# Window attention scores as 64x64 matmuls on quarters of the TensorE array: two heads per matmul in place of four

## The chip, the cores and the metric

The kernel runs on one core of one Trainium2 chip. The metric is device time in microseconds (us) of one execution; lower is better. Each kernel was run on the same chip, in the same rounds, as the kernel before. Engines are written as in the profile: PE is TensorE, PEld its weight loads, DVE VectorE, ACT ScalarE, POOL GpSimd. "Cold" means that the clock record of the trace shows a granted TensorE clock of 0.50, "warm" that it shows 1.00; the 264 records of the trace before have no other value. The 263 changes of the clock inside the span stand within 3 ns of a grid of 3413.33 ns; a step of that grid is called a clock window here, or a window.

## The reference

There are 32 images of 56x56 positions and 128 channels, all fp32. Two layers follow each other, each with a group norm in front and a residual around it.

```python
# layer 0: shifted-window attention, 64 windows of 7x7 = 49 tokens, 4 heads of 32
qkv  = (win @ w_qkv.T).reshape(-1, 49, 3, 4, 32)
attn = einsum('bhid,bhjd->bhij', q * 32**-0.5, k) + bias + shift_mask
out  = einsum('bhij,bhjd->bihd', softmax(attn), v) @ w_proj.T + b_proj
...
# layer 1: cosine transform along rows and along columns, 32 modes each with its own
# 128x128 matrix, transform back, sum; then a feed-forward 128 -> 512 -> 128
out_y = einsum('bixy,ioy->boxy', dct(x)[..., :32], w0)
...
h = relu(h @ W1 + b1) @ W2 + b2
```

## The kernel before

An image's attention goes by eight rows of eight windows. From the second image on it runs beside layer 1 of the image before; a scheduler decides the order of instructions on each engine. The scores use keys laid out block-diagonally: head h's keys stand in channels 32h to 32h+31 and in columns of their own, with zeros elsewhere, so one matmul on all 128 channels gives all four heads of a window.

```python
k_bd = big.tile([P, NWR, NH, WT], F32, ...)          # 128 x 8 x 4 x 49, zeros written once
...
for h in range(NH):                                  # 4 copies a row, two engines in turn
    hs = slice(h * HD, (h + 1) * HD)
    if h % 2: nc.vector.tensor_copy(k_bd[hs, :, h], pk3[hs])     # L244
    else:     nc.scalar.copy(k_bd[hs, :, h], pk3[hs])            # L246
...
for hf in range(2):
    ps = attn_bank()
    for w4 in range(4):
        w = 4 * hf + w4
        half = w % 2
        nc.tensor.matmul(                            # L270: scores
            ps[half * JP : (half + 1) * JP, ...],    # JP = 64: two windows, one per column half
            lhsT=q[:, w * WT : w * WT + JP],         # 128 x 64
            rhs=k_bd[:, w].rearrange("c h j -> c (h j)"),   # 128 x 196
            start=True, stop=True)
```

In layer 1 the part that matters is the mode matrices (L405), in a first group of 32 matmuls (with `w1sb`) and, later in the image, a second group (with `w0sb`). In front of each the group norm's shift is added to the constant mode, and in front of the second GpSimd adds a bias to a large tile:

```python
nc.vector.tensor_scalar(y[:, 0], y[:, 0], shift, None, ALU.add)             # L394
if width:                                                                    # second group only
    nc.gpsimd.tensor_tensor(xtok, xtok, b2sb..., ALU.add)                    # L396
for g in range(NM // 8):
    pz = conv_bank()
    for c in range(8):
        nc.tensor.matmul(pz[:, c * S : (c + 1) * S], lhsT=wmix[:, k], rhs=y[:, k], ...)   # L405
```

## Time and profile before

| kernel before | value | from |
|---|---|---|
| time | 6739.01 us, median of 3 (6730.82 to 6739.05) | first runs |
| profiled span, mean granted clock | 6717.8 us, 0.882 | profile |
| time with the clock at 0.50 | 1591 us | clock record |
| scores: 2048 matmuls, 4096 passes | 506.8 us busy, 272.2 us idle in front | groups |
| second mode groups that stay cold | 9 of 31 | timeline of TensorE |

The prediction shows the page's lines and the timeline. An fp32 matmul is recorded as two passes, so a count of x16 in a timeline is eight matmuls. The stall in front of the second mode group is in the timeline of all engines (start, us, engine, line, operation, tiles and shapes, count, and in brackets the idle time before with what ended it):

```profile
2716.82 7.73 POOL L396 TENSOR_TENSOR xtok<-xtok,b2sb 112x3584 f32<-112x3584 f32 x1 [6.26 <-PE pc L379]
2717.23 7.37 DVE L394 TENSOR_SCALAR y<-y,shift 128x56 f32<-128x56 f32 x1 [0.59 <-ACT y L388]
```

A VectorE addition on 56 elements a partition takes 7.37 us. The same instruction takes 250 ns at its fastest, ahead of the first mode group, where GpSimd does not run its large addition; here it lasts until that addition ends (2724.60 and 2724.55 us). TensorE waits for it, and the clock record falls to 0.50 at 2720.20 us.

### The profile page before, as it was taken

How to read it: one execution, taken by the hardware profiler on the slowest of the kernel's cores; microseconds unless marked ns; L12 is line 12 of the kernel's file. 1: busy time of each engine (PE TensorE's matmuls, PEld its weight loads, DVE VectorE, ACT ScalarE, POOL GpSimd, SP SyncE). 2: the span in 40 equal slices, each digit the busy share in tenths (PEclk: the TensorE clock that was granted, in tenths of full speed). 3: DMA queues.
4: the chain of work that ended last, by engine and by line, in shares of the span. 5: the costliest groups of instructions: out<-in, count | busy, mean ns of one | idle time of the engine just before them, and what ended most of it. 6: DMA issues, size and time to landing. Idle time of an engine off the chain costs nothing.

```text
span 6717.8 us, 106748 instructions
## 1 busy us (share of the span) xinstructions
PE 5716.7 (85%) x46336; PEld 4468.3 (67%) x46336; DVE 2547.3 (38%) x4263; ACT 2529.2 (38%) x4737; POOL 1637.8 (24%) x1614
## 2 busy tenths in 40 slices
PE   5888889888888888898888888888888888888888
PEld 3766667666667666676666766666766667666666
DVE  4343333333343433333333334334343333333331
ACT  2433334334334343343333343433433334334332
POOL 2222221222212222212222122222122221222210
PEclk8988889889898898898898998988988989889886
DMA  1000000000000000000000000000000000000000
GB/s 57 13 15 19 20 20 11 15 16 20 20 17 12 13 20 20 20 11 13 17 20 20 11 16 15 20 20 20 9 13 19 20 20 11 15 16 20 11 11 10
DMA packets 210798, 115.20 MB, mean 17 GB/s; under 512 B 7927, under 2 KB 209944, under 8 KB 210072
## 3 DMA queue, kind: packets, MB, share of 16 engines
q1 hardware_dynamic: 206136, 102.84, 5.9%
q8 instruction: 364, 5.96, 0.4%
q10 hardware_dynamic: 4192, 5.54, 0.2%
q14 instruction: 106, 0.87, 0.0%
HBM read 56.93 MB, written 51.38 MB: 16 GB/s over the span
## 4 chain that ended last, share of the span: by engine, by line
PE 68%; DVE 12%; POOL 9%; ACT 8%; issue 2%; DMA 0%; SPq 0%; ACTq 0%; POOLq 0%; DVEq 0%
PE pc L464 11%; PE pc L405 9%; PE pc L450 9%; PE pa L270 7%; PE pc L379 7%; PE pc L433 6%; POOL xw L218 6%; DVE y L394 4%; PE pa L329 3%; PE pa L316 3%; PE pa L306 3%; PE pa L239 2%; PE pa L236 2%; POOL t L288 2%; PE pa L251 2%
## 5 line engine op out<-in xcount | busy, mean ns | idle before, releaser
L288 POOL TENSOR_TENSOR t<-t,mx 128x784 f32<-128x784 f32 x256 | 384.2, 1501 | 3506.8 <-DVE mx L287 3506.8
L464 PEld LDWEIGHTS pc<-wff,hid 128*112 128x112 f32 x7168 | 844.2, 177 | 142.3 <-issue 69.3
L464 PE MATMUL pc<-wff,hid 128*112 128x128 f32 x7168 | 897.3, 275 | 1.8
L458 ACT ACTIVATE hid<-pc,b1sb 128x448 f32<-128x448 f32 x896 | 549.5, 632 | 686.7 <-PE pc L450 650.7
L270 PE MATMUL pa<-k_bd,q 128*64 128x196 f32 x4096 | 506.8, 380 | 272.2 <-DVE k_bd L244 272.2
L450 PE MATMUL pc<-xf,wff 128*128 128x448 f32 x1792 | 728.6, 541 | 0.0
L244 DVE COPY k_bd<-pa 32x392 f32<-32x392 f32 x512 | 289.5, 566 | 910.6 <-ACT k_bd L246 908.6
L296 POOL TENSOR_TENSOR a<-a,rs 128x784 f32<-128x784 f32 x256 | 388.6, 1518 | 826.9 <-DVE rs L295 561.0
L270 PEld LDWEIGHTS pa<-k_bd,q 128*64 128x64 f32 x4096 | 337.8, 157 | 359.1 <-DVE k_bd L244 267.1
L405 PE MATMUL pc<-y,w0sb 128*128 128x56 f32 x2048 | 380.1, 371 | 230.1 <-DVE y L394 230.1
L405 PEld LDWEIGHTS pc<-y,w0sb 128*128 128x128 f32 x2048 | 370.1, 284 | 253.3 <-DVE y L394 241.3
L312 DVE COPY aT<-pa 128x512 f32<-128x512 f32 x512 | 352.8, 689 | 471.2 <-PE pa L306 469.9
L277 DVE TENSOR_TENSOR t<-pa,bm 128x392 f32<-128x392 f32 x512 | 289.9, 567 | 630.0 <-PE pa L270 622.7
L316 PE MATMUL pa<-aT,v 128*64 128x49 f32 x8192 | 385.2, 239 | 120.1 <-DVE aT L312 120.1
L316 PEld LDWEIGHTS pa<-aT,v 128*64 128x64 f32 x8192 | 315.4, 149 | 250.1 <-DVE aT L312 134.0
L450 PEld LDWEIGHTS pc<-xf,wff 128*128 128x128 f32 x1792 | 318.6, 191 | 213.9 <-issue 208.1
L388 ACT ACTIVATE y<-pc,rstd 128x256 f32<-128x256 f32 x448 | 211.5, 472 | 613.0 <-PE pc L379 459.3
L472 DVE TENSOR_TENSOR xtok<-pc,xtok 112x512 f32<-112x512 f32 x224 | 154.4, 689 | 746.2 <-PE pc L464 746.2
L412 ACT COPY z<-pc 128x448 f32<-128x448 f32 x256 | 136.2, 532 | 779.0 <-PE pc L405 779.0
L306 PE MATMUL pa<-ident,a 128*128 128x128 f32 x2048 | 369.5, 306 | 48.0 <-POOL a L296 48.0
L334 DVE SCALAR_TENSOR_TENSOR xT<-pa,bproj,xT 128x371 f32<-128x371 f32 (+2 forms) x576 | 200.2, 394 | 492.5 <-PE pa L329 492.5
L218 POOL TENSOR_SCALAR xw<-xT,rstd,nb 128x343 f32<-128x343 f32 (+7 forms) x864 | 370.9, 450 | 11.9 <-DVE ve L174 11.5
(78 smaller groups left out, 8916.5 us busy)
## 6 DMA issues: line engine op xcount, KB each, us to landing
xload<-in_x_dram SPq DMA_DIRECT2D x64, 784.0 KB
out_dram<-xtok SPq DMA_DIRECT2D x224, 224.0 KB
w0sb<-in_w_dram ACTq DMA_DIRECT2D x1, 2048.0 KB
w1sb<-in_w_dram ACTq DMA_DIRECT2D x1, 2048.0 KB
wff<-in_W_dram ACTq DMA_DIRECT2D x2, 256.0 KB
rpb<-in_rpb_rev_dram ACTq DMA_DIRECT2D x25, 0.8 KB
rpb<-in_rpb_rev_dram SPq DMA_DIRECT2D x24, 0.8 KB
wqkv<-in_w_qkv_t_dram ACTq DMA_DIRECT2D x1, 192.0 KB
```

The source lines that it names most:

```text
L218: nc.gpsimd.tensor_scalar(xw[:, i, j0:j1, r0:r1, s0:s1], xT[:, y0 : y0 + r1 - r0, x0 : x0 + cols].rearrange("p r (j s) -> p j r s", s=s1 - ...
L270: nc.tensor.matmul(ps[half * JP : (half + 1) * JP, (w4 // 2) * NH * WT : (w4 // 2 + 1) * NH * WT], lhsT=q[:, w * WT : w * WT + JP], rhs=k_ ...
L288: nc.gpsimd.tensor_tensor(t3, t3, mx.unsqueeze(2).to_broadcast([P, NR, WT]), ALU.subtract)
L296: nc.gpsimd.tensor_tensor(a3, a3, rs.unsqueeze(2).to_broadcast([P, NR, WT]), ALU.mult)
L306: nc.tensor.transpose(pt[:, m * P : (m + 1) * P], a[:, pr, 2 * hp : 2 * hp + 2].rearrange("p h j -> p (h j)"), ident,)
L316: nc.tensor.matmul(po[hp * JP : (hp + 1) * JP, w * WT : (w + 1) * WT], lhsT=v[:, w, hp].rearrange("j h d -> j (h d)"), rhs=aT[:, 2 * (w4 / ...
L379: nc.tensor.matmul(py[:, c * 2 * NM : (c + 1) * 2 * NM], lhsT=tok[:, c], rhs=dct_sb, start=True, stop=True,)
L405: nc.tensor.matmul(pz[:, c * S : (c + 1) * S], lhsT=wmix[:, k], rhs=y[:, k], start=True, stop=True,)
L433: nc.tensor.matmul(px[:, c * NL : (c + 1) * NL], lhsT=zT[:, c], rhs=idct, start=True, stop=True)
L450: nc.tensor.matmul(ph[:, :GT], lhsT=wff1[:, f * P : (f + 1) * P], rhs=xf[:, 8 * g : 8 * g + 8].rearrange("p r w -> p (r w)"), start=True, ...
L458: nc.scalar.activation(hf, ph[:, :GT], AF.Relu, bias=b1sb[:, f : f + 1])
L464: nc.tensor.matmul(pf[:TC, c * C : (c + 1) * C], lhsT=hid[f][:, c * TC : (c + 1) * TC], rhs=wff2[:, f], start=(f == 0), stop=(f == NF - 1),)
```

## The change

The intent is to halve the array work of the scores. Heads 0 and 1 lie in channels 0 to 63, heads 2 and 3 in 64 to 127. A matmul on one half of the channels needs only two heads' columns: 64 rows, 64 columns of the array, 98 streamed columns. Two halves of the channels and two windows make four quarters of the array; that they work at the same time was not shown before the change, and is measured below (24 ns a pass on four quarters in turn, 43 on two). The keys shrink to 128 x 8 x 2 x 49, the scores of a head pair go to a PSUM bank of their own, and the bias tile, `t` and `a` are regrouped to fit. The numbers of copies, additions and softmax steps stay.

```diff
-    k_bd = big.tile([P, NWR, NH, WT], F32, tag="k_bd", name="k_bd")
+    k_bd = big.tile([P, NWR, 2, WT], F32, tag="k_bd", name="k_bd")
...
-        for hf in range(2):
-            ps = attn_bank()
-            for w4 in range(4):
-                w = 4 * hf + w4
-                half = w % 2
+        ps = [attn_bank(), attn_bank()]
+        for w in range(NWR):
+            for hp in range(2):
+                cs = slice(hp * JP, (hp + 1) * JP)
+                qs = slice((w % 2) * JP, (w % 2 + 1) * JP)
                 nc.tensor.matmul(
-                    ps[half * JP : (half + 1) * JP, (w4 // 2) * NH * WT : (w4 // 2 + 1) * NH * WT],
-                    lhsT=q[:, w * WT : w * WT + JP],
-                    rhs=k_bd[:, w].rearrange("c h j -> c (h j)"),
+                    ps[hp][qs, (w // 2) * 2 * WT : (w // 2 + 1) * 2 * WT],
+                    lhsT=q[cs, w * WT : w * WT + JP],
+                    rhs=k_bd[cs, w].rearrange("c h j -> c (h j)"),
                     start=True,
                     stop=True,
                 )
...
```

Cut: the layouts of the bias tile, `t`, `a` and the transposes of `a`, which follow from this, and comments. Line numbers move: scores L270 are L276 after, key copies L244/L246 are L248/L250, mode matrices L405 are L412, the shift's addition L394 is L401, attention times values L316 is L323.

More of the change, by code (lines that the diff above doesn't have):

```diff
@@ L121, in swin_fourier_kernel @@
     mask_sb = const_load([P, 2, 3, WT], shift_mask.rearrange("r s p j -> p r s j"), "mask")
-    bm = const.tile([P, 2, 3, NH, WT], F32, tag="bm", name="bm")
-    rpb_f = rpb.rearrange("p h y x -> p h (y x)")
+    bm = const.tile([P, 2, 2, NWR // 2, 2, WT], F32, tag="bm", name="bm")
+    rpb_f = rpb.rearrange("p (t h) y x -> p t h (y x)", t=2)
     for r in range(2):
-        for s in range(3):
-            nc.vector.tensor_tensor(
-                bm[:, r, s],
-                rpb_f,
-                mask_sb[:, r, s].unsqueeze(1).to_broadcast([P, NH, WT]),
-                ALU.add,
-            )
+        for pr in range(NWR // 2):
+            for t in range(2):
+                nc.vector.tensor_tensor(
+                    bm[:, r, t, pr],
+                    rpb_f[:, t],
+                    mask_sb[:, r, 0 if pr < NWR // 2 - 1 else 2]
+                    .unsqueeze(1)
+                    .to_broadcast([P, 2, WT]),
+                    ALU.add,
+                )
     dct_sb = const_load([TC, 2 * NM], dct, "dct")
@@ L151, in swin_fourier_kernel @@
         v_bd.append(big.tile([P, NWR, 2, 2, HD], F32, tag=f"v{i}", name=f"v{i}"))
-        a_sb.append(big.tile([P, NWR // 2, NH, JP], F32, tag=f"a{i}", name=f"a{i}"))
+        a_sb.append(big.tile([P, 2, NWR // 2, 2, JP], F32, tag=f"a{i}", name=f"a{i}"))
         nc.gpsimd.memset(q_sb[i], 0.0)
@@ L243, in attn_scores @@
             if h % 2:
-                nc.vector.tensor_copy(k_bd[hs, :, h], pk3[hs])
+                nc.vector.tensor_copy(k_bd[hs, :, h % 2], pk3[hs])
             else:
-                nc.scalar.copy(k_bd[hs, :, h], pk3[hs])
+                nc.scalar.copy(k_bd[hs, :, h % 2], pk3[hs])
         pv = attn_bank()
@@ L263, in attn_scores @@
             )
-        t = work.tile([P, 2, 2, NH * WT], F32, tag="t", name="t")
-        for hf in range(2):
-            ps = attn_bank()
-            for w4 in range(4):
-                w = 4 * hf + w4
-                half = w % 2
+        t = work.tile([P, 2, RT], F32, tag="t", name="t")
+        ps = [attn_bank(), attn_bank()]
[3 more added lines that the diff above has]
+                qs = slice((w % 2) * JP, (w % 2 + 1) * JP)
                 nc.tensor.matmul(
-                    ps[half * JP : (half + 1) * JP, (w4 // 2) * NH * WT : (w4 // 2 + 1) * NH * WT],
-                    lhsT=q[:, w * WT : w * WT + JP],
-                    rhs=k_bd[:, w].rearrange("c h j -> c (h j)"),
+                    ps[hp][qs, (w // 2) * 2 * WT : (w // 2 + 1) * 2 * WT],
+                    lhsT=q[cs, w * WT : w * WT + JP],
+                    rhs=k_bd[cs, w].rearrange("c h j -> c (h j)"),
                     start=True,
@@ L276, in attn_scores @@
                 )
+        for hp in range(2):
             nc.vector.tensor_tensor(
-                t[:, hf],
-                ps[:, : 2 * NH * WT].rearrange("p (a m) -> p a m", a=2),
-                bm[:, i // (NWR - 1), hf : hf + 2].rearrange("p a h j -> p a (h j)"),
+                t[:, hp],
+                ps[hp][:, :RT],
+                bm[:, i // (NWR - 1), hp].rearrange("p a h j -> p (a h j)"),
                 ALU.add,
@@ L283, in attn_scores @@
         NR = NWR // 2 * NH
-        t3 = t.rearrange("p f a (h j) -> p (f a h) j", h=NH)
-        a3 = a.rearrange("p a h j -> p (a h) j")[:, :, 0:WT]
+        t3 = t.rearrange("p t (m j) -> p (t m) j", j=WT)
+        a3 = a.rearrange("p t a h j -> p (t a h) j")[:, :, 0:WT]
         mx = small.tile([P, NR], F32, tag="mx", name="mx")
@@ L307, in attn_out @@
                     pt[:, m * P : (m + 1) * P],
-                    a[:, pr, 2 * hp : 2 * hp + 2].rearrange("p h j -> p (h j)"),
+                    a[:, hp, pr].rearrange("p h j -> p (h j)"),
                     ident,
```

## The prediction

> **What bounds the kernel now.** I read the page first (engines, granted clock, chain that ended last), then the groups by shape, then TensorE's instructions in order of time over several images. The kernel handles 32 images; from the second on, an image's attention runs beside the previous image's Fourier layer and feed-forward.
>
> ```profile
> PE   5888889888888888898888888888888888888888
> PEclk8988889889898898898898998988988989889886
> PE 68%; DVE 12%; POOL 9%; ACT 8%; issue 2%; DMA 0%; SPq 0%; ACTq 0%; POOLq 0%; DVEq 0%
> L270 PE MATMUL pa<-k_bd,q 128*64 128x196 f32 x4096 | 506.8, 380 | 272.2 <-DVE k_bd L244 272.2
> L251 PE MATMUL pa<-wqkv,xw 128*49 128x64 f32 x8192 | 322.4, 229 | 0.0
> L316 PE MATMUL pa<-aT,v 128*64 128x49 f32 x8192 | 385.2, 239 | 120.1 <-DVE aT L312 120.1
> ```
>
> TensorE is the bound: 68% of the chain, busy nearly everywhere. The scores (L270) hold 7% of the chain, some 470 us; that is the ceiling of what the change can touch. The second row matters as much: the mean granted clock is 0.882. Read microsecond by microsecond it is only ever 0.50 or 1.00, and 1591 us of the span (about 49 us an image) are at 0.50. The page's last column of L270 says TensorE also stood idle 272 us in front of it, waiting for the key copies.
>
> The timeline of TensorE shows where the clock comes back:
>
> ```profile
> 2724.66 7.07 PE L405 MATMUL pc<-y,w0sb 128*128 128x56 f32 x32 [7.17 <-DVE y L394]
> 2731.66 2.60 PE L270 MATMUL pa<-k_bd,q 128*64 128x196 f32 x14
> 2734.19 3.78 PE L405 MATMUL pc<-y,w0sb 128*128 128x56 f32 x32
> ...
> 3752.36 7.07 PE L405 MATMUL pc<-y,w0sb 128*128 128x56 f32 x32 [7.17 <-DVE y L394]
> 3759.37 2.88 PE L270 MATMUL pa<-k_bd,q 128*64 128x196 f32 x14
> 3762.17 7.08 PE L405 MATMUL pc<-y,w0sb 128*128 128x56 f32 x32
> ...
> 6631.52 13.90 PE L405 MATMUL pc<-y,w0sb 128*128 128x56 f32 x64 [7.96 <-DVE y L394]
> ```
>
> (Start, us, instructions; an fp32 matmul is recorded as two passes.) Each image TensorE idles 7.2 us for the shift (DVE, L394) and the clock falls to half. Sixty-four passes of the mode matrices follow; 14 score passes stand in their middle. In 22 of the 31 images with attention the second 32 passes take 3.78 us (full clock), in 9 they take 7.08. In the last image, without attention and so without a score burst, all 64 stay cold. The dense burst is what wakes the clock, and a lone stretch of L405 does not: cold, a pass takes 221 ns and streams 56 of its columns for some 94. Image periods are 204.8 to 205.2 us after a woken burst and 207.8 to 208.1 after a failed one.
>
> [...]With window edges fitted to the observed clock changes, the burst covers 1.7 us of the window in two failed cases, about 1.88 in one that failed and one that worked, 2.0 in the working example above; with L405 at 43% density beside it, the threshold is some three quarters (an estimate from the trace). [...]16 score passes take (1.55 - 0.33) / 15 = 81 ns each, while a 448-column pass takes 376 ns, 0.84 ns a column, so 196 columns alone would take 165; two halves already overlap fully. Nothing shows row groups yet. [...]The trace has gaps of about 0.1 us where L251, L270 and L464 alternate[...].
>
> **The change, part by part.** The arithmetic of scores is halved: per row of windows, 8 matmuls of 196 columns and 128 rows become 16 of 98 columns and 64 rows. On paper 4 quarters at once give 98 x 0.84 / 4 = 21 ns a pass. But L251 and L316, of 64 and 49 columns on 64-wide halves, run at (1.10 - 0.22) / 31 = 28 and (0.67 - 0.22) / 15 = 30 ns a pass, which looks like a floor[...]. So 32 x 28 = 0.90 us against 16 x 82 = 1.31: 0.41 us warm, twice that cold. Over 31 x 8 rows that would be about 120 us, 1.8%.
>
> The built order does not allow that. The listing of the changed program shows who is next to whom. A is a matmul on heads 0-1, B on heads 2-3, a dot is other work between:
> 93 rows AAAAAAAA.BBBBBBBB; 39 rows AAAAAAAABBBBBBBB; 31 each of AAA.AAAABBBBBBBAB, AB.ABABABABABABAB, ABABA.BABABABABAB, AAAAABBBBBABABAB.
> The A matmuls need only the first two key copies, so the scheduler puts them first. A run of A alone uses one row half: 98 x 0.84 / 2 = 41 ns a pass, 32 of them 1.31 us, no gain. Only two rows of eight are interleaved, a third partly.
>
> Per image, in warm time:
> - Rows really interleaved: row 3 saves 0.4, row 5 about 0.2. Row 4 is the burst in the shift's stall: 22 passes x 28 = 0.6 instead of 14 x 82 = 1.15, so 0.55. Together 1.15 us saved.
> - Starting A before the last keys: TensorE waits 0.88 us in row 2 and 1.25 in row 7, and 5.99 in row 0. A's 0.66 us fits into each wait. I count 0.5 and 0.6, and 0.25 in row 0, where a group of transposes moves from the wait to behind it. Together 1.35 us saved.
> - [...]The value matmuls (128 x 64 mode) are followed by 64 x 64 mode, and six rows are split by other work instead of two: some 8 extra changes x 0.1 = 0.8 us lost.
> - VectorE's two additions, 0.567 us each, and softmax are of equal size; key copies 4 a row as before. In interleaved rows both additions wait for the end, 0.1 to 0.2 us later, hidden under Fourier work.
> Sum: 1.7 us saved an image.
>
> Against it, the clock. The remaining burst in the stall is 22 passes x about 50 ns cold (L316 and L251 show 50) = 1.1 us. One window holds then at most (1.1 + 2.3 x 0.43) / 3.41 = 0.6 of activity, below three quarters. So all 31 images should behave as the 9 do now: 207.9 us instead of the mean (6431.51 - 256.52) / 30 = 205.8 from first L405 to first L405. That is +2.1 us. Row 0's cold restart may move by a window either way: now the 2.81 us score burst wakes the clock there in the later-phase images; afterwards the two 392-column projections, which come 1.5 us sooner, must do it. A window costs 1.7 us; I take +0.4 as the mean.
> Net per image: -1.7 + 2.1 + 0.4 = +0.8 us, x 31 = +25 us: 6739 + 25 = 6764, I say 6765.
>
> **The rivals.**
> 1. The paper gain arrives: quarters overlap across the breaks too, or the burst still wakes the clock. For: TensorE is the bound and L270 is on the chain. Against: the order, and the last image's cold 13.90 us. It would save 1.7 us an image with no loss, 53 us: 6685; with all rows interleaved and waits gone, 6610.
> 2. Clock loss with phases falling badly: the images settle at 61 windows of 3.413, 208.2 us, +2.4 x 31 = 74: 6813; a further lost window an image gives 6866. For: periods already sit at 60 windows. Against: less work before each edge should slip some images back to 60.
> 3. Row halves do not overlap or a quarter's pass has a higher floor: the interleaved rows cost 32 x 41 as the others, 1.15 us less gain, about 6800.
> 4. [...]0.2 us: another 0.8 us an image, about 6790.
> Nothing speaks for a new bound on another engine: VectorE and ScalarE are at 38%.
>
> **Range and chances.** The gain of 53 us and the clock loss of 65 to 80 us nearly cancel, and the window quantization makes either larger by up to 1.7 us an image (53 us). Range 6675 to 6845. Faster by over 2% needs below 6604, beyond even rival 1: 0.04. Slower by over 2% needs above 6874, rivals 2 and 4 together: 0.05. Within 2%: 0.91.
>
> **What would show it.** Right: after the shift's stall, both groups of 32 mode passes at 7 us in nearly all images, the score burst between them near 1.1 us, cold time rising from 1591 us by several hundred; the score groups with start spacing 28 to 30 ns where interleaved and about 41 where A runs alone; idle before the scores falling from 272 us. Wrong: the second mode group still 3.78 us in most images (then rival 1), or A runs at 80 ns a pass (then tiles of 64 x 64 don't overlap by columns), or image periods under 204.

The forecast's sum: 1.15 + 1.35 - 0.8 = 1.7 us saved an image, and -1.7 + 2.1 + 0.4 = +0.8 us, 6765 us in all. The 0.1 us for a change of tile, in the term of 0.8, is in the trace before: passes of L464 (tile 128*112) start 109 ns after one another, and the first pass of L251, L270 or L316 (tiles 128*49 and 128*64) behind one of L464 starts 203 ns after it. Behind L251 the first score pass starts 50 ns after the last in the trace before and 149 in the trace after (tile 64*64). Rival 4 takes that change at 0.2 us. On the grid of the whole trace the burst, up to the next pass of L405, fills at best 1.85 to 2.11 us of one window in the nine failed images and 2.12 to 2.48 in the 22 woken ones.

## The result, and the profile after

The changed kernel takes 6821.86 us (median of 4, 6806.51 to 6832.37) beside 6734.91 us for the kernel before. Ratios are the mean time of one kernel's runs over that of the other's of the same rounds, so not quite the ratio of the medians: 1.0128, 95% interval 1.0112 to 1.0144. That is within 2%, in the range, but 1.3% slower where 0.4% was predicted.

The page of the profile after: TensorE busy in tenths of 40 slices, the granted clock in the same slices, the engines' shares of the chain that ended last, and the group of the scores (busy us, mean ns of one; idle before).

```profile
PE   5988989888898888898888988888888889888888
PEclk8988888888888888898888887888888889889886
PE 73%; DVE 12%; POOL 8%; ACT 5%; issue 2%; DMA 0%; SPq 0%; ACTq 0%; POOLq 0%; DVEq 0%
L276 PE MATMUL pa<-k_bd,q 64*64 64x98 f32 x8192 | 448.3, 272 | 172.2 <-DVE k_bd L248 168.0
```

The scores' busy time falls from 506.8 to 448.3 us and the idle time that the keys cause from 272.2 to 168.0 us. TensorE's share of the chain rises all the same. The second row says why: eights where there were nines, a mean of 0.849 instead of 0.882. Cold time rises from 1591 to 2060 us, by 469 us. The span grows by 85.5 us.

The timeline of TensorE around the second mode group (columns as above):

```profile
4004.69 7.07 PE L412 MATMUL pc<-y,w0sb 128*128 128x56 f32 x32 [7.02 <-DVE y L401]
4011.70 1.25 PE L276 MATMUL pa<-k_bd,q 64*64 64x98 f32 x22
4012.88 7.07 PE L412 MATMUL pc<-y,w0sb 128*128 128x56 f32 x32
```

The score burst is 1.25 us instead of 2.6 to 2.9, and the 32 passes behind it need 7.07 us: cold. It is so in all 31 images with attention; before it was so in 9.

Where the time went is best seen by cutting an image, from one first mode group to the next, into five stretches between starts of matmuls, and averaging each over 29 images of a trace. In each cell: us, and in brackets how much of it is cold.

| stretch | before, 20 woken images | before, 9 failed images | before, all 29 | after, all 29 |
|---|---|---|---|---|
| 1: first mode group | 6.97 (0) | 6.97 (0) | 6.97 (0) | 7.41 (0.9) |
| 2: to the second mode group, with the stall | 45.22 (4.4) | 45.27 (4.7) | 45.24 (4.5) | 45.06 (5.8) |
| 3: second mode group | 13.07 (9.2) | 16.47 (16.5) | 14.12 (11.5) | 14.84 (14.8) |
| 4: to the last feed-forward matmul | 73.44 (0) | 75.64 (6.2) | 74.13 (1.9) | 76.27 (6.3) |
| 5: to the next first mode group | 66.24 (30.7) | 63.56 (24.3) | 65.41 (28.7) | 65.37 (34.5) |
| period | 204.94 | 207.92 | 205.86 | 208.96 |

Stretch 5 holds the output of window row 7, the next image's transposes and normalization, and row 0. A failed burst in the kernel before costs 3.40 us in stretch 3 and 2.20 in stretch 4 but gives 2.68 back in stretch 5, where the clock is cold 6.4 us less. In the changed kernel every burst fails, stretches 3 and 4 show it, and stretch 5 gives little back: it takes 65.37 us against 66.24 after a woken burst, and 34.5 us of it are cold.

### The profile page after: what moved, and what is told of

Same layout as the page of the kernel before. It is cut to its first block, busy times and chain, and to the rows that moved or that the text cites. A ratio compares the mean times of both kernels' runs of the same rounds, so it can differ in the third digit from the quotient of the medians.

```text
span 6803.3 us, 114850 instructions
## 1 busy us (share of the span) xinstructions
PE 5858.0 (86%) x50432; PEld 4643.2 (68%) x50432; DVE 2526.6 (37%) x4273; ACT 2542.5 (37%) x4737; POOL 1639.9 (24%) x1614
## 4 chain that ended last, share of the span: by engine, by line
PE 73%; DVE 12%; POOL 8%; ACT 5%; issue 2%; DMA 0%; SPq 0%; ACTq 0%; POOLq 0%; DVEq 0%
PE pc L471 12%; PE pc L412 10%; PE pc L457 10%; PE pc L386 6%; PE pc L440 6%; POOL xw L222 5%; PE pa L276 5%; PE pa L323 5%; DVE y L401 3%; PE pa L336 3%; PE pa L313 3%; PE pa L255 3%; PE pa L243 3%; PE pa L240 2%; PE pc L376 2%; DVE aT L319 2%
## 5 line engine op out<-in xcount | busy, mean ns | idle before, releaser
L412 PE MATMUL pc<-y,w0sb 128*128 128x56 f32 x2048 | 452.5, 421 | 225.5 <-DVE y L401 225.5
L248 DVE COPY k_bd<-pa 32x392 f32<-32x392 f32 x512 | 289.2, 565 | 882.1 <-ACT k_bd L250 879.2
L412 PEld LDWEIGHTS pc<-y,w0sb 128*128 128x128 f32 x2048 | 441.5, 332 | 238.8 <-DVE y L401 231.6
L276 PE MATMUL pa<-k_bd,q 64*64 64x98 f32 x8192 | 448.3, 272 | 172.2 <-DVE k_bd L248 168.0
L323 PE MATMUL pa<-aT,v 128*64 128x49 f32 x8192 | 415.2, 250 | 165.4 <-DVE aT L319 165.4
L323 PEld LDWEIGHTS pa<-aT,v 128*64 128x64 f32 x8192 | 339.2, 159 | 309.7 <-DVE aT L319 186.1
L276 PEld LDWEIGHTS pa<-k_bd,q 64*64 64x64 f32 x8192 | 346.9, 146 | 226.6 <-DVE k_bd L248 188.8
L313 PE MATMUL pa<-ident,a 128*128 128x128 f32 x2048 | 400.1, 318 | 27.8 <-POOL a L303 27.7
L222 POOL TENSOR_SCALAR xw<-xT,rstd,nb 128x343 f32<-128x343 f32 (+7 forms) x864 | 373.1, 452 | 11.9 <-DVE ve L178 11.5
```

The source lines that it names most:

```text
L222: nc.gpsimd.tensor_scalar(xw[:, i, j0:j1, r0:r1, s0:s1], xT[:, y0 : y0 + r1 - r0, x0 : x0 + cols].rearrange("p r (j s) -> p j r s", s=s1 - ...
L276: nc.tensor.matmul(ps[hp][qs, (w // 2) * 2 * WT : (w // 2 + 1) * 2 * WT], lhsT=q[cs, w * WT : w * WT + JP], rhs=k_bd[cs, w].rearrange("c h ...
L313: nc.tensor.transpose(pt[:, m * P : (m + 1) * P], a[:, hp, pr].rearrange("p h j -> p (h j)"), ident,)
L323: nc.tensor.matmul(po[hp * JP : (hp + 1) * JP, w * WT : (w + 1) * WT], lhsT=v[:, w, hp].rearrange("j h d -> j (h d)"), rhs=aT[:, 2 * (w4 / ...
```

## The experiments

The theory after the result: the clock does not count how long TensorE is busy but how much of the array works, so scores on quarters are worth less to it, and the kernel pays in cold time. The rivals: the new order and the waits that it makes; changes of tile and the passes' own cost; chance of the phase between images and clock windows.

### before_half_rows: the kernel before, with scores on 64 rows only

```diff
-                    lhsT=q[:, w * WT : w * WT + JP],
-                    rhs=k_bd[:, w].rearrange("c h j -> c (h j)"),
+                    lhsT=q[JP:P, w * WT : w * WT + JP],
+                    rhs=k_bd[JP:P, w].rearrange("c h j -> c (h j)"),
```

The scores of heads 0 and 1 are wrong (their bias alone is left; the output stayed within tolerance). The order of instructions is that of the kernel before, one for one, with the same number of passes and columns. The rows of the array that work are halved, and with them the tile becomes 64x64 in place of 128x64; what that change of tile costs by itself is measured below, where there is no stall.

> The kernel before, with each score matmul on rows 64 to 127 of the array only (same columns, same count, same order, same waits; wrong result on purpose). Theory (the clock follows the filled share of the array: rows x columns x streaming over 3.41 us): the burst in the stall counts half, about 0.5 against a threshold of some 0.73, so all 31 second groups of mode passes stay at 7.07 us, cold time rises from 1591 us to 2000 or more, and the time rises by 2 to 4% (6870 to 7000 us). Rival 1 (the clock follows the time TensorE is busy, and the change lost it by making the burst shorter): this burst is as long as before, so 22 of 31 groups stay at 3.78 us and the time is within 0.3% of 6735.

Measured: 6891.26 us, ratio to before 1.0258 [1.0243, 1.0274], slower than the change itself. Its timeline of TensorE at the second mode group:

```profile
3006.36 7.07 PE L405 MATMUL pc<-y,w0sb 128*128 128x56 f32 x32 [7.02 <-DVE y L394]
3013.36 2.87 PE L270 MATMUL pa<-k_bd,q 64*64 64x196 f32 x14
3016.16 7.07 PE L405 MATMUL pc<-y,w0sb 128*128 128x56 f32 x32
```

Fourteen passes in 2.87 us, as before, and the clock does not wake, here nor in any other image. The tail of an image shows the other half. First the kernel before, row 7 of an image whose burst had failed too:

```profile
3847.59 1.55 PE L270 MATMUL pa<-k_bd,q 128*64 128x196 f32 x16 [1.25 <-DVE k_bd L244]
3849.07 0.66 PE L306 MATMUL pa<-ident,a 128*128 128x128 f32 x4
3850.60 0.67 PE L316 MATMUL pa<-aT,v 128*64 128x49 f32 x16 [0.87 <-DVE aT L312]
```

Then half rows:

```profile
3101.58 1.54 PE L270 MATMUL pa<-k_bd,q 64*64 64x196 f32 x16 [1.25 <-DVE k_bd L244]
3103.06 1.11 PE L306 MATMUL pa<-ident,a 128*128 128x128 f32 x4
3105.05 1.10 PE L316 MATMUL pa<-aT,v 128*64 128x49 f32 x16 [0.88 <-DVE aT L312]
```

The scores take the same 1.5 us with the same wait in front. In the first the transposes behind them run at 0.66 us, and the clock record falls at 3856.84; in the second it falls at 3103.05, and they take 1.11. The two excerpts do not stand at the same place of the grid on which the clock changes (every 3413 ns): row 7's scores begin 0.99 us after a grid line in the first and 1.94 us in the second. The whole traces settle whether the place makes the difference. In the kernel before, 20 images have these scores 1.87 to 2.24 us after a grid line, and the clock falls 8.0 to 8.4 us after they begin. With half rows, five images have them 1.88 to 1.96 us after one, and it falls after 1.45 to 1.53 us.

Against the nine failed images of before, the stretches are 6.97, 45.47, 16.46, 76.23 and 66.11 us (35.9 of it cold), period 211.24: of the 3.3 us a period more, 2.55 lie in stretch 5. The third rival, chance of the phase, can be checked in the same way. In four kernels with the old scores (before, before_wake, before_fill, before_nostall) stretch 5 takes 63.4 to 64.2 us in 65 of the 67 images in which it begins 0.3 to 1.6 us after a grid line, and 65.9 to 66.5 us in the 49 in which it begins 1.7 to 3.4 us after one. So the place counts, and the nine failed images all begin at a good one, 1.09 to 1.45. With half rows no place is good: all 29 images take 65.4 to 66.8 us. So the rows that work count, in the stall and in the tail, and the theory holds for this kernel.

### after_inter: the changed kernel, with the two head pairs in turn

```diff
-        for w in range(NWR):
-            for hp in range(2):
+        mm = None
+        for w, hp in [(w, hp) for w in range(NWR) for hp in (1, 0)]:
...
+                with tc.issue_after(mm.ins) if mm is not None else nullcontext():
```

The built order then has ABAB throughout in 225 of 256 rows and with one break in the other 31, so all four quarters can overlap (24 ns a pass, below); if the order of the change were at fault, this would be faster.

> The changed kernel with the score matmuls forced to alternate between the two row halves in every row of windows. Theory (clock): score passes 24 to 28 ns in all rows, but the burst still too thin, all second groups 7.07 us; the early start of the first half is lost; ratio to before 1.00 to 1.02. Rival 2 (the loss is the scheduler's order: lost overlap[...]): the paper gain comes back, ratio 0.98 to 0.99.

Measured: 6852.41 us (6841.87 to 6908.83), ratio 1.0217 [1.0175, 1.0260]: a little above the expected range, unclear by the 2% rule, and slower than the changed kernel's 1.0128. A pass in turn costs (0.89 - 0.244) / 27 = 24 ns against (0.89 - 0.244) / 15 = 43 where one head pair runs alone, in these two lines of the changed kernel's own timeline (0.244 us is the median of one pass):

```profile
3890.20 0.89 PE L276 MATMUL pa<-k_bd,q 64*64 64x98 f32 x16
...
3980.56 0.89 PE L276 MATMUL pa<-k_bd,q 64*64 64x98 f32 x28
```

The overlap is real, and cheaper passes did not make a faster kernel, so lost overlap is not the loss. The order is not cleared by this run, though. The forced order also waits for the last keys and puts a projection between the matmuls of the first mode group, which takes 8.01 us instead of 7.25 in 30 of 31 images; stretch 2 is 0.74 us longer than in the changed kernel, and stretch 5 is 0.99 us shorter (64.38 us).

### before_nostall and after_nostall: both kernels without the stall

```diff
-            nc.vector.tensor_scalar(y[:, 0], y[:, 0], shift, None, ALU.add)
+            nc.scalar.activation(y[:, 0], y[:, 0], AF.Identity, bias=shift)
```

If the stall's lost wake-ups are the loss, the change should gain once the stall is gone.

> The kernel before with the shift added by ScalarE instead of VectorE, so that the 7.4 us wait beside the GpSimd addition goes and with it the clock drop there. Theory: no cold time around the second mode group, about 13 us an image saved (7 of idle, 6.5 of 18 cold us at half speed), ratio 0.93 to 0.96. If it were slower or same, the stall would not be what drops the clock.

> The changed kernel with the same edit. Theory (clock): without the stall the burst has nothing to wake, so most of the loss goes: against before_nostall 0.985 to 1.000 in time (tail still somewhat colder, scores cheaper). Rival 2 (order[...]): it stays 1.2% slower than before_nostall.

Measured: before_nostall 6260.05 us, ratio 0.9319 [0.9305, 0.9333]; after_nostall 6309.13 us, ratio 0.9393 [0.9378, 0.9409]. The clock row of before_nostall's page, and the moved addition's line from its groups by shape:

```profile
PEclk8998999999999999999999999999999999999996
L394 ACT ACTIVATE y<-y,shift 128x56 f32<-128x56 f32 x64 | 21.8, 341 | 1.1
```

The addition costs 341 ns in the mean, beside a GpSimd addition that still takes 7.77 us; the second mode group is warm and takes 8.02 us in stretch 3. This one line gains 6.8%, about as much as the whole group of scores holds of the chain (7%). But the expectation for the pair was missed: with the change, the kernel is still 0.9393 / 0.9319 = 1.008 of the one without. Its stretches differ from those of before_nostall by +0.88, +0.16, -0.32, +0.52 and +0.57 us. The median period is the same, 191.14 and 191.17 us, both 56.0 clock windows of 3.4133 us; the mean differs because 12 of the 29 periods are longer with the change, most of all the four whose first mode group is cold (199 to 202 us). So the stall is not all of it.

### half_rows_nostall and inter_nostall: what remains without the stall

The edits are those above, combined.

> before_nostall with the scores on half of the rows (wrong on purpose). It asks what the rest of after_nostall's loss is, 0.8%. Theory: it is the thinner activity too (a clock drop in front of the first mode group in some images, a colder tail), so this kernel, which has none of the change's new order[...], also loses against before_nostall: 0.4 to 1.5%. If the rest is the order[...], it is within 0.2% of before_nostall.

> after_inter with the stall removed: all rows interleaved, 24 ns a pass, no stall to wake from. If the scores' time on TensorE still counted, it would beat before_nostall (0.932) by up to 1%; by the theory the periods lock to whole clock windows and the thinner activity costs about what is saved: ratio to before 0.930 to 0.945.

Measured: half_rows_nostall 6351.09 us, 0.9457 [0.9441, 0.9473], 1.0148 times before_nostall (in other rounds); inter_nostall 6317.47 us, 0.9398 [0.9379, 0.9418], as after_nostall. Half rows make the period 2.54 us longer than before_nostall's, and 2.02 of it is stretch 5 (35.6 us cold instead of 30.8), with the order unchanged. The thinner scores thus cost time in rows 7 and 0 even where there is no stall. Stretches 2 and 4 show what is not the clock's, since they are warm throughout in both kernels: they are 0.38 and 0.15 us longer. Most of that, 0.45 us, stands where the scores and the values' matmuls (L251, tiles of 128x64) follow each other: the first score pass starts 149 ns after the last pass of L251 instead of 50. A change of tile costs about 0.10 us here.

### after_wake and before_wake: a dense burst put where the score burst was

Two matmuls without use, of 448 columns on the whole array, into a bank that the next ones overwrite.

```diff
             for g in range(NM // 8):
                 pz = conv_bank()
+                for _ in range(2 if width and g == 2 else 0):
+                    nc.tensor.matmul(
+                        pz[:, : 8 * S],
+                        lhsT=wff1[:, :P],
+                        rhs=y[:, :8].rearrange("p k s -> p (k s)"),
+                        start=True,
+                        stop=True,
+                    )
```

> The changed kernel plus two useless dense matmuls (448 columns, whole array, 4 passes, some 3 us cold) right behind the score burst in the shift's stall; their result is overwritten. Theory: the burst is then full enough again, nearly all second groups of mode passes take 3.78 us, the cold stretch there shrinks from 24 to 27 us to 14 to 17, and despite 3 us more of work an image the time falls: ratio to before 0.995 to 1.005. If the loss is not the clock's, the 3 us an image come on top: 1.025 or more.

> The control of after_wake: the kernel before with the same two dense matmuls behind its score burst. Theory: all second groups at 3.78 us (9 cold ones mended, worth some 1 us an image), 2 to 3 us of work added an image: ratio to before 1.000 to 1.012, so that after_wake at 0.9936 is 0.7 to 1.8% faster than it: this is what the cheaper scores are worth once the clock in the stall is settled. If the change had no gain to give, the two would be equal.

Measured: after_wake 6672.38 us, ratio to before 0.9936 [0.9921, 0.9951], so about 0.9936 / 1.0128 = 0.981 of the changed kernel (in other rounds) although TensorE has more to do. Its timeline of TensorE:

```profile
3121.03 7.08 PE L420 MATMUL pc<-y,w0sb 128*128 128x56 f32 x32 [7.02 <-DVE y L401]
3128.04 1.25 PE L276 MATMUL pa<-k_bd,q 64*64 64x98 f32 x22
3129.22 3.35 PE L411 MATMUL pc<-y,wff 128*128 128x448 f32 x4
3132.37 3.82 PE L420 MATMUL pc<-y,w0sb 128*128 128x56 f32 x32
```

The four added passes cost 3.35 us and the second half of the group saves 3.25: stretch 3 is 14.85 us, as without them. The gain is behind: stretch 4 falls from 76.27 us (6.3 cold) to 73.13 (0 cold). That is 3.14 of the 4.04 us by which the mean period falls, from 208.96 to 204.92; the first mode group, cold in no image now, gives another 0.44.

before_wake: 6742.63 us, but two runs near 6702 and two near 6790, ratio 1.0036 [0.9965, 1.0108]. The kept trace is of the run of 6782 us: of its 29 periods the first four are 204.7 to 204.8 us, 60 clock windows, and the last 24 are 208.0 to 208.4 us, 61 windows. If the two faster runs stayed at 60 windows, that would account for the gap between the pairs, some 89 us or 26 windows; no trace of them was kept. So the middle of the four says little: the change with the burst is about 0.4% faster than the two faster runs of before_wake and 1.7% faster than the two slower ones (in other rounds). That the cheaper scores are worth something once the stall's clock is settled looks likely, and its size stays open.

### after_fill, before_fill and nostall_fill0: dense work ahead of the cold place

Nine such matmuls (operand `w0sb`, ready early) at `g == 0`, so that they run in the stall itself; in nostall_fill0, five ahead of row 0's scores, on top of before_nostall.

```diff
+                for _ in range(9 if width and g == 0 else 0):
...
+                        rhs=w0sb[:, :4].rearrange("p k c -> p (k c)")[:, : 8 * S],
```

> The changed kernel with nine useless dense matmuls (6.8 us) in the shift's stall, where TensorE idles: the stall stays, the clock should not drop. Theory: both mode groups at 3.8 us, cold time in the stall from 26 to under 5 us an image, ratio to before 0.95 to 0.98, and within 1% of before_fill. If the idle time of the stall rather than the clock were what counts, nothing is gained.

> The kernel before with the same nine matmuls. Theory: cold time in the stall from 18 to under 5 us an image, ratio to before 0.96 to 0.98; after_fill then no more than 1% from it, since what is left apart is the thinner clock activity in the other places and the cheaper scores.

> An attempt at a still better kernel: before_nostall with five useless dense matmuls in the 6 us in which TensorE waits for the keys of an image's first row of windows, so that the clock does not drop there. If the cold stretch of some 7 to 10 us in row 0 goes: 0.915 to 0.930. If the filler runs cold itself and delays the row, 0.935 or more.

Measured: after_fill 6687.92 us, 0.9954 [0.9939, 0.9969]; before_fill 6611.82 us, 0.9850 [0.9830, 0.9871]. Both gain less than expected. In after_fill stretch 3 is nearly warm, 8.68 us (0.4 cold), but the cold has moved: the first mode group is cold in 19 of 29 images, and stretch 1 has a mean of 11.13 us. In before_fill stretch 3 is still 12.38 us (7.2 cold). nostall_fill0 takes 6280.91 us, 0.9342 [0.9328, 0.9356], no better than before_nostall: cold time in stretch 5 falls from 30.8 to 24.4 us but the stretch does not get shorter, 64.15 and 64.54 us. Ten added passes are 3.8 us warm, and 6.5 us less of cold save 3.2 at most, so the dense work paid for no more than itself.

### What the clock counts: an estimate from the traces

For each window between two lines of the grid of 3413 ns I summed over TensorE's passes the columns streamed, at 0.84 ns a column warm (376 ns for 448 in the trace before) and 1.68 cold (in the trace after, passes of 224 columns start 189 ns apart warm and 373 cold), times the share of rows and the share of columns of the array in use. In the trace before, cold windows wake above 0.72 to 0.73 of a full window (2 of 466 on the wrong side), and warm ones stay warm above 0.31 (2 of 1481). With busy time in place of that sum, 38 or more of the 466 are on the wrong side, by how busy time is counted. In before_half_rows the sum misplaces some 13 of 633 and busy time 98 or more. In the changed kernel's trace the borders come out at some 0.75 and 0.35, with up to 19 of 603 and 22 of 1372 on the wrong side, so they are known to a few hundredths only. For a window that holds the whole burst of the stall it gives, with the mode passes' 0.43 (94 of 221 ns) in the rest:

| kernel | burst: passes x columns x 1.68 ns x share of array | best window | wakes |
|---|---|---|---|
| before | 14 x 196 x 1.68 x 1/2 = 2.31 us in 2.60 | (2.31 + 0.81 x 0.43) / 3.41 = 0.78 | 22 of 31 |
| before_half_rows | 14 x 196 x 1.68 x 1/4 = 1.15 us in 2.87 | (1.15 + 0.54 x 0.43) / 3.41 = 0.41 | never |
| after | 22 x 98 x 1.68 x 1/4 = 0.91 us in 1.25 | (0.91 + 2.16 x 0.43) / 3.41 = 0.54 | never |
| after_wake | 4 x 448 x 1.68 = 3.01 us in 3.35 | (3.01 + 0.06 x 0.72) / 3.41 = 0.90 | always |

## Why the prediction was wrong

**What held.** TensorE stayed the bound and no other engine became one. The order kept the quarters apart in most rows. A head pair alone runs at 43 ns a pass (41 predicted), in turn at 24 (28 predicted). The burst shrank to 1.25 us (1.1 predicted), all 31 second groups are cold at 7.07 us, idle time before the scores fell, and cold time rose by several hundred microseconds. The direction, slower, was right too.

**The step that failed** is "So all 31 images should behave as the 9 do now: 207.9 us instead of the mean". The 207.9 us of the nine failed images is a sum in which stretch 5 gives 2.68 us back. That return was taken over unseen into the +2.1 us. It comes with the old scores, where stretch 5 begins 0.3 to 1.6 us after a grid line, as it does in all nine. Against those nine images the changed kernel measures, stretch by stretch, +0.44, -0.21, -1.63, +0.63 and +1.81 us, together +1.04, where the prediction's own terms (-1.7 and +0.4) make -1.3. The miss of 2.3 us an image is thus mostly stretch 5: about -0.3 by my terms for the waits of rows 7 and 0, the phase and a share of the changes of tile, +1.81 measured. before_half_rows shows what takes the return away: in the same order, with passes as long and half the rows, stretch 5 is 2.55 us longer with 11.6 us more of it cold, wherever it begins. In the changed kernel the rows are not all: 20 of its images begin stretch 5 at 1.23 to 1.68 us, where the old scores nearly always take 63.4 to 63.8, and take 65.57 in the mean; but seven begin at 1.98 to 2.27 and take 64.5 us, less than the old scores there (66.2). How much of the +1.81 is the thinner scores and how much the new order, no run separates.

**The smaller misses.** The prediction had the clock matter in the stall alone. It also falls before or in the first mode group of a few images (0.44 us in the mean). Two such images of the changed kernel have periods of 219 us. One shows in the timeline of TensorE; all 31 groups of the kernel before take 7.25 us there:

```profile
1860.34 13.74 PE L412 MATMUL pc<-y,w1sb 128*128 128x56 f32 x64
```

That no half-row kernel has a cold first group, and that the changed kernel, after_fill and after_nostall have, points to the new order and not to the rows, though after_wake, in the same order, has none; by the estimate above the thinnest stretch in the 8 us ahead of that group falls from 0.41 to 0.31 with the change and stays at 0.41 with half rows. No run isolates it. In stretch 4 without stalls, 0.52 us are lost where row 5 was to gain 0.2. The traces show where: TensorE's idle time in it grows from 0.85 to 1.48 us an image, because in the new order the transform back along the width waits longer for ScalarE's copies (before_nostall, then after_nostall, groups by shape):

```profile
L433 PE MATMUL pc<-idctw,zT 128*128 128x224 f32 x896 | 224.5, 373 | 10.1 <-ACT zT L430 3.5
L440 PE MATMUL pc<-idctw,zT 128*128 128x224 f32 x896 | 228.9, 379 | 36.6 <-ACT zT L437 34.1
```

So the new order does cost time, by waits that the prediction did not look for.

**The saved work** of 1.7 us an image was too hopeful. In the pair without stalls the warm part of stretch 2 is 0.47 us shorter in the median, stretch 3 is 0.32 shorter and stretch 4 is 0.52 longer, so about 0.3 us of the saving is seen, and none of it shows in the median period, which stays at 56.0 windows.

**The rivals.** The second came nearest: "the images settle at 61 windows of 3.413, 208.2 us", which it put at 6813 us. The median period of the changed kernel is 208.19 us by the cut above, and the time is 6822 us. But the images do not settle there: 27 periods lie anywhere from 206.8 to 210.0 us and two near 219, so the size was right and the picture of it was not. What spoke against it, that less work would slip images back to 60 windows, did not happen in any image. The first rival, the gain on paper, did not come with full overlap either: after_inter is slower, and inter_nostall no faster than after_nostall. The third is refuted by the 24 ns, which also lie below the 28 ns that the prediction took for a floor. The fourth is not seen: a change of tile costs 0.10 us (149 ns instead of 50 between the values' passes and the scores, in half_rows_nostall and in after_nostall), as the prediction had it, and not 0.2.

## What to carry to other kernels

Before counting what a TensorE change saves, read the granted clock: cutting the array work of small matmuls can cost more than it saves, where those matmuls were what woke or held the clock, as here (1.28% slower, with the scores' busy time down by 58 us). Do not take a clock's cost from whole periods; cut the period into stretches, since one failure may be paid back elsewhere by something that the change removes. Work saved need not show in the period at all: 20 of 29 periods of the kernel before are 204.8 to 205.2 us, and 60 windows are 204.8; without the stall the median is 191.14 us, and with the change 191.17, both 56 windows; before_wake has 24 of 29 at 61. It is no rule: half rows give 211.24 us, 61.9 windows. And look first for the wait that drops the clock: moving one 250 ns addition off VectorE gained 6.8% here, while the rework of the scores lost 1.3%.
